# A graph-network kernel on one core: layer 0's mask bytes written to DRAM by casting transfers instead of GpSimd casts

## The chip, the core and the metric

The kernel runs on one core of one Trainium2 chip, as one launch. The metric is the device time of that launch in microseconds, the median of several runs. A profile of one execution, taken by the hardware profiler, goes with it.

The engines are named as the profile names them: PE is TensorE (matmuls; PEld is its weight loads), DVE is VectorE, ACT is ScalarE, POOL is GpSimd, SP is SyncE, which here only issues DMAs. "q" after an engine's name is its instruction queue. The DMA queue of GpSimd is q0 (software_dynamic), that of SyncE is q1 (hardware_dynamic); both are served by the same 16 DMA engines.

## The reference

`x` is 2708 x 512 float32, `adj` is a symmetric 2708 x 2708 matrix of zeros and ones with about 16 ones in a row. Four layers follow one another, each of the form `x = layernorm(x + layer(x, adj))`:

```python
deg = max((adj != 0).sum(-1), 1)
# layer 0
pooled = (dinv * (adj + I) * dinv) @ x + x        # dinv = rsqrt(deg)
relu(pooled @ W + b)
# layer 1
dis = (adj.sum(1) + 1e-8) ** -0.5
(dis * adj * dis) @ x @ W.T + b
# layer 2: twice
Wh, Ws = split(x @ W)
a = softmax(Wh @ Ws.T) * adj
leaky_relu(a @ Wh + x)
# layer 3
adj @ (H @ W) + b
```

## The kernel before

The 2708 nodes are cut into 22 blocks of 128 rows (the last has 20), and the columns of the transposed adjacency matrix into six chunks `CH` of 512, 512, 512, 512, 384 and 276 columns. The 22 blocks of a chunk go in six groups `GROUPS` of 4, 4, 4, 4, 3 and 3 blocks. Layers 0, 1 and 3 multiply by the adjacency matrix in steps (layer, chunk, group): for each block j of the group, a 128-row piece of `x`, split into a high part `xh` and a rest `xl`, is the stationary operand, and the piece `m` of `adj.T` (128 rows, one chunk of columns) is the moving one. The products of a chunk gather in four PSUM banks `acc`. Layer 2 is the attention. It has its own loops and uses the stored masks too.

The order of instructions on each engine is the order in which the program issues them; it is written out by hand, by `Run.seq` and `step`. `step` of a group first calls `before_products`, which issues the loads of the group two steps ahead (`load`), the preparation of the next group (`prepare`), and at two places the column sums (`degrees`). Then it issues the matmuls of the group (`multiply`). After the last group of a chunk come `degrees` and `evict`. The chunk's second product (`project`, matmuls into `mm`), its end and its layernorm (`ends`) are spread over the steps of the next chunk.

What layer 0 does with a block of `adj.T`:

- `load`: SyncE loads it as float32 into a tile `at`, one of eleven wide buffers. In chunk 0 GpSimd also loads the block of `x`; in the third group of each chunk it loads four tiles `xt` of the transposed input.
- `prepare`: ScalarE splits `x` into `xh` (`halve`, chunk 0 only; VectorE makes `xl`), and casts `at` to the moving operand `m`.
- `examine`: ScalarE casts two blocks `at` into one bfloat16 tile `some`; VectorE compares every block with itself (`odd`, with a count of the entries that are not zero or one) and adds the pair to a running sum `part`. The bytes of the group are stored in DRAM, in `masks[k]`, laid out as 128 partitions x 22 blocks x chunk width. Layers 1 to 3 load their adjacency from there, at a quarter of the bytes.
- `degrees`: after the last block VectorE adds the halves of `part` (`both`), TensorE sums them over the partitions (`deg`, `cnt`), VectorE makes `dg` and from `cnt` in a string of small instructions (`rs_v`, `rs_y`, `rs_t`) `dis` and `rdeg`; GpSimd multiplies the four tiles `xt` by `dg`.
- `evict`: VectorE adds `acc` and `xt` into `ht`, the stationary operand of `mm`.

The storing of the bytes, before: for each pair of blocks GpSimd casts `some` to a `uint8` tile `bytes`; after the group's pairs, one DMA issued by GpSimd stores the tile. GpSimd's queue at the start therefore holds, in order: loads of `x` for the first groups, constants, and then for each group its two casts, the store, the loads of `x` of a later group, and between them the loads of `xt`, of the weights `w` and of the bias.

Nearly all SBUF tiles come from one pool of 82 pages, each as large as 128 x 512 float32; a tile takes a free page when it is made, and waits for that page's last user. `bytes`, `some`, `odd` and `part` are pages, the `at` tiles are not.

All instructions are recorded through one wrapper, so that most of the profile's rows show its line, L70, and have to be told apart by the tiles' names.

Of the kernel before, what the change touches and what calls it, by code (L numbers as in the profile page):

```python
# [12 lines left out]
U8 = mybir.dt.uint8  # L13
# [6 lines left out]
P = 128  # L20
# [4 lines left out]
DC = D // P  # L25
BANK = 512
# [487 lines left out]
class Fast:  # L514
# [299 lines left out]
    def examine(self, ly, k, g, ats):  # L814
        nc, cw = self.nc, CH[k][1]
        b0 = GROUPS[g][0]
        if g == 0:
            ly.part[k] = self.page(f"part{k}", BF, (P, 2, BANK))
        odd = self.page(f"odd{k}_{g}", BF)
        at_b = self.page(f"bytes{k}_{g}", U8, (P, DC, BANK))  # L820
        for q in range(0, len(ats), 2):
            some = self.page(f"some{k}_{g}_{q}", BF, (P, 2, BANK))
            m = min(2, len(ats) - q)
            for h in range(m):
                at = ats[q + h][:, :cw]
                n = k * NB + b0 + q + h
                nc.scalar.copy(some[:, h, :cw], at)
                nc.vector.scalar_tensor_tensor(
                    odd[:, :cw],
                    at,  # L830
                    1.0,
                    at,
                    ALU.is_equal,
                    ALU.not_equal,
                    accum_out=self.k.bad[:, n : n + 1],
                )
            nc.gpsimd.tensor_copy(at_b[:, q : q + m, :cw], some[:, :m, :cw])

            n = QW if b0 + q == NB - 1 else P
            p, t = ly.part[k][:n, :m, :cw], some[:n, :m, :cw]  # L840
            if b0 + q == 0:
                nc.vector.tensor_copy(p, t)
            else:
                nc.vector.tensor_add(p, p, t)
        nc.gpsimd.dma_start(
            self.k.masks[k][:, b0 : b0 + len(ats), :], at_b[:, : len(ats), :cw]
        )

    def multiply(self, ly, k, g, only=None, ds=range(DC)):
        nc, cw = self.nc, CH[k][1]  # L850
# [993 lines left out]
```

## Time and profile before

| what | value |
|---|---|
| median of 3 runs | 2369.26 us (2368.26 to 2371.22) |
| the profiled execution: time / span | 2338.2 us / 2336.5 us |
| mean granted TensorE clock in it | 0.993 |
| layer 0, from the first instruction to its last mask store | about 0 to 316 us |
| GpSimd casts `bytes<-some` | 72, 75.4 us |
| GpSimd DMA issues `mask<-bytes` | 36, 22.3 us |
| time from issue to landing of these | 2.3 to 5.7 us, median 3.6 |
| DMA of the whole kernel | 463.5 MB, mean 198 GB/s |

The profile's times come from its one execution; its own time stands beside its span. A row of a group names the engine, the operation, the tiles (out<-in) with their shapes and count, then the busy time in microseconds and the mean of one in nanoseconds, and after the bar the idle time ahead of the group and what ended it. A row of the waits reads: engine, tile and line, then what it waited for, the total in microseconds, the number of times and the longest. A row of stages gives for each engine the busy microseconds and the number of instructions.

### The profile page before, as it was taken

The numbers are of one execution on the slowest core, as the hardware profiler recorded it, in microseconds if no ns is written. First come the engines' busy times: TensorE is split into PE (matmuls) and PEld (weight loads), VectorE is DVE, ScalarE is ACT, GpSimd is POOL, SyncE is SP. The second block draws the span as 40 slices with busy tenths as digits, with TensorE's granted clock in tenths as the row PEclk, the third lists the DMA queues.
The fourth block names the chain that finished last, engine by engine and source line by source line (L and its number), as shares of the span: only waits on it lengthen the run. The fifth ranks groups of instructions, "written<-read, shape, count | busy, mean of one in ns | idle before, by whom it ended". The sixth has DMA issues, their size and how long they took to land.

```text
span 2336.5 us, 26171 instructions
## 1 busy us (share of the span) xinstructions
PE 2274.8 (97%) x8518; PEld 1292.5 (55%) x8518; DVE 1474.8 (63%) x2831; ACT 662.2 (28%) x1334; POOL 762.3 (33%) x879
## 2 busy tenths in 40 slices
PE   8999999999999999999999999999999999999997
PEld 6677677778644444443456444444443456566585
DVE  6999986786655529657677511228677788724523
ACT  6544353223100113222223200113232334432211
POOL 6645641111000000636375550000636466551000
PEclk9999999999999999999999999999999999999998
DMA  9765652222434404869699996405869799983311
GB/s 343 258 199 169 182 172 86 74 86 70 171 146 167 154 0 143 278 229 311 204 324 350 302 388 232 152 0 163 279 217 314 233 316 329 305 279 96 123 48 43
DMA packets 312440, 463.50 MB, mean 198 GB/s; under 512 B 60162, under 2 KB 189706, under 8 KB 312292
## 3 DMA queue, kind: packets, MB, share of 16 engines
q1 hardware_dynamic: 252276, 240.81, 31.5%
q0 software_dynamic: 60016, 220.92, 27.1%
q8 instruction: 69, 1.13, 0.2%
q14 instruction: 79, 0.65, 0.1%
HBM read 307.75 MB, written 153.85 MB: 198 GB/s over the span
## 4 chain that ended last, share of the span: by engine, by line
PE 84%; DVE 7%; DMA 4%; issue 2%; ACT 1%; POOL 1%; SPq 0%; DVEq 0%; ACTq 0%; POOLq 0%
PE sp L70 32%; PE acc L70 29%; PE mm L70 9%; PE z L70 6%; PE wst L70 6%; DMA pairs<-s 1%; DMA at<-in_adj_t 1%; DVE st L70 1%; DMA at<-mask 1%; ACT m L70 1%; DVE s L70 1%; PE list L70 1%; PE mix L70 0%; POOL bytes L70 0%; PE tr_x2t L70 0%
## 5 line engine op out<-in xcount | busy, mean ns | idle before, releaser
L70 POOL DMA_INDIRECT g<-pairs,givers x510 | 516.2, 1012 | 897.0 <-DMA pairs<-s 537.4
L70 PE MATMUL sp<-xs,wst_sb 128*128 128x512 f32 (+3 forms) x2112 | 797.7, 544 | 0.0
L70 PEld LDWEIGHTS sp<-xs,wst_sb 128*128 128x128 f32 (+1 forms) x2112 | 380.0, 186 | 406.8 <-issue 321.9
L70 PE MATMUL acc<-m,xh 128*128 128x512 f32 (+4 forms) x1584 | 571.4, 382 | 13.6 <-ACT m L70 7.0
L70 PE MATMUL acc<-m,xl 128*128 128x512 f32 (+4 forms) x1584 | 553.2, 367 | 1.5 <-DVE xl L70 1.5
L70 PEld LDWEIGHTS acc<-m,xh 128*128 128x128 f32 (+1 forms) x1584 | 290.3, 189 | 81.4 <-issue 22.3
L70 PEld LDWEIGHTS acc<-m,xl 128*128 128x128 f32 (+1 forms) x1584 | 290.3, 189 | 48.1 <-issue 5.7
L70 ACT COPY s<-sp 128x512 f32<-128x512 f32 (+2 forms) x252 | 133.6, 531 | 482.1 <-PE sp L70 469.5
L70 PE MATMUL acc<-g 128*32 128x512 f32 (+1 forms) x1020 | 260.8, 605 | 0.9 <-DMA g<-pairs,givers 0.5
L70 DVE TENSOR_TENSOR top<-top,s 128x512 f32<-128x512 f32 (+5 forms) x240 | 149.6, 623 | 170.6 <-ACT s L70 169.1
L70 PE MATMUL mm<-w,ht 128*128 128x512 f32 (+1 forms) x528 | 222.6, 593 | 8.1 <-DVE ht L70 8.1
L70 ACT CAST m<-at 128x512 fp32r<-128x512 uint8 (+5 forms) x396 | 199.2, 567 | 80.0 <-DMA at<-mask 63.7
L70 ACT ACTIVATE s<-s 128x512 f32<-128x512 f32 (+3 forms) x264 | 150.7, 580 | 236.6 <-DVE s L70 236.3
L70 DVE TENSOR_TENSOR sum<-sum,s 128x512 f32<-128x512 f32 (+4 forms) x252 | 157.4, 625 | 23.9 <-ACT s L70 23.9
L70 DVE TENSOR_TENSOR s<-s,a 128x512 f32<-128x512 f32 (+3 forms) x264 | 165.9, 628 | 10.2 <-DMA a<-mask 1.2
L70 DVE TENSOR_TENSOR s<-s,shift 128x512 f32<-128x512 f32 (+3 forms) x264 | 162.8, 620 | 6.7 <-ACT shift L70 6.7
L70 PEld LDWEIGHTS mm<-w,ht 128*128 128x128 f32 (+1 forms) x528 | 95.5, 186 | 124.4 <-issue 110.9
L70 PE MATMUL wst<-xt,mixed 128*128 128x512 f32 (+2 forms) x384 | 152.5, 550 | 1.7 <-ACT mixed L70 1.7
L70 PEld LDWEIGHTS acc<-g 128*32 128x32 f32 (+1 forms) x1020 | 75.4, 134 | 136.9 <-issue 115.8
L70 PE MATMUL z<-w,xt 128*128 128x512 f32 (+1 forms) x352 | 151.0, 596 | 0.0
L70 DVE COPY z_sb<-z 128x512 f32<-128x512 f32 (+1 forms) x44 | 30.3, 690 | 179.5 <-PE z L70 176.3
L70 POOL DMA_DIRECT2D x<-o x44 | 26.0, 596 | 358.0 <-DVE o L70 354.2
(167 smaller groups left out, 1657.4 us busy)
## 6 DMA issues: line engine op xcount, KB each, us to landing
pairs<-s SPq DMA_DIRECT2D x378, 128.0 KB
pairs<-z_sb SPq DMA_DIRECT2D x84, 512.0 KB
at<-in_adj_t SPq DMA_DIRECT2D x84, 256.0 KB
xres<-x POOLq DMA_DIRECT2D x44, 256.0 KB, 4.3
x<-o POOLq DMA_DIRECT2D x43, 256.0 KB, 3.1
x<-x SPq DMA_DIRECT2D x37, 256.0 KB
at<-mask SPq DMA_DIRECT2D x32, 256.0 KB
xt<-t SPq DMA_DIRECT2D x32, 256.0 KB
```

The source lines that it names most:

```text
L70: ins = call(*args, **kw)
```

## The change

In `examine` the tile of bytes is no longer made, and GpSimd's cast is gone. In its place GpSimd issues a DMA for each pair of blocks straight from the bfloat16 tile `some` to the `uint8` tensor in DRAM; the transfer converts each element. The store of the whole group behind the loop is gone. So a group has two transfers where it had one, each of two blocks (or one, where a group has three).

```diff
@@ examine
         odd = self.page(f"odd{k}_{g}", BF)
-        at_b = self.page(f"bytes{k}_{g}", U8, (P, DC, BANK))
         for q in range(0, len(ats), 2):
             some = self.page(f"some{k}_{g}_{q}", BF, (P, 2, BANK))
...
-            nc.gpsimd.tensor_copy(at_b[:, q : q + m, :cw], some[:, :m, :cw])
+
+            nc.gpsimd.dma_start(
+                self.k.masks[k][:, b0 + q : b0 + q + m, :], some[:, :m, :cw]
+            )
...
                 nc.vector.tensor_add(p, p, t)
-        nc.gpsimd.dma_start(
-            self.k.masks[k][:, b0 : b0 + len(ats), :], at_b[:, : len(ats), :cw]
-        )
```

## The prediction, made before the change was run

> **What bounds the kernel now.** I read the page's engine shares first, then the waits of TensorE, then the stage in which the edited function runs (layer 0, up to about 320 us), and there the wait that ends last.
>
> ```profile
> PE 2274.8 (97%) x8518; PEld 1292.5 (55%) x8518; DVE 1474.8 (63%) x2831; ACT 662.2 (28%) x1334; POOL 762.3 (33%) x879
> PE 84%; DVE 7%; DMA 4%; issue 2%; ACT 1%; POOL 1%; SPq 0%; DVEq 0%; ACTq 0%; POOLq 0%
> ```
>
> TensorE (PE) fills 97% of the span and 84% of the chain; GpSimd (POOL), from which the change takes work, carries 1% of the chain. So the change is worth what it does to TensorE's few gaps. The waits of TensorE from 0 to 60 us, and then from 60 to 360 us:
>
> ```profile
> PE mix L70 <- DMA wt<-in_w_t: 4.3, 1, 4.3
> PE acc L70 <- ACT m L70: 3.5, 2, 2.9
> ```
>
> ```profile
> PE mm L70 <- DVE ht L70: 5.5, 3, 2.3
> PE acc L70 <- DVE dg L70: 3.6, 1, 3.6
> PE acc L70 <- DVE xl L70: 1.2, 1, 1.2
> ```
>
> That is all that can come back: 2.95 us at 59.2 (m late), then 2.26, 1.25 and 1.95 us at 75.8, 235.1 and 279.8 (ht late), and 3.57 us at 312.95 (dg late). The table of stages says what stands behind them (TensorE, weight loads, VectorE (DVE), ScalarE (ACT), POOL, granted clock, DMA share, GB/s):
>
> ```profile
> 21.00:24.00 3.00, 3.00 (x14) 2.44 (x14) 2.96 (x6) 3.00 (x7) 2.70 (x4) 1.00 0.30 100
> 24.00:39.00 15.00, 15.00 (x68) 12.40 (x67) 14.86 (x29) 12.05 (x25) 11.79 (x20) 1.00 0.99 346
> 39.00:50.00 11.00, 11.00 (x49) 8.81 (x47) 10.15 (x15) 6.74 (x14) 8.88 (x11) 1.00 1.04 398
> 61.00:64.20 3.20, 3.20 (x9) 2.52 (x8) 3.10 (x6) 3.20 (x7) 2.69 (x4) 0.50 1.01 362
> 116.00:172.00 56.00, 56.00 (x231) 39.82 (x230) 53.52 (x105) 23.55 (x46) 28.26 (x35) 1.00 0.62 196
> 313.40:317.00 3.60, 3.60 (x11) 2.77 (x10) 2.19 (x7) 3.60 (x7) 2.84 (x6) 0.53 0.96 356
> ```
>
> Three things are to be seen. From 24 to 60 us the DMA engines are full; that is what the first gap waits for. Later the DMA is at 0.62 and VectorE is the runner-up, busy 53.5 of 56 us. And after the two longest gaps (2.95 and 3.57 us) the granted clock is halved for some 3.5 us, so each costs about 1.8 us more than itself; the shorter ones cost nothing further.
>
> VectorE's groups up to 345 us, and the tile odd alone:
>
> ```profile
> L70 DVE SCALAR_TENSOR_TENSOR odd<-at 128x512 bf16<-128x512 f32 x88 | 88.1, 1001 | 1.4
> L70 DVE TENSOR_TENSOR part<-part,some 128x1024 bf16<-128x1024 bf16 x36 | 34.6, 961 | 0.2 <-ACT some L70 0.2
> ```
>
> ```profile
> L70 DVE SCALAR_TENSOR_TENSOR odd<-at x132: 431/688/3196, 19.1 to 305.6; 128x512 bf16<-128x512 f32 x88, 128x384 bf16<-128x384 f32 x22, 128x276 bf16<-128x276 f32 x22
> ```
>
> The first gives a mean of 1001 ns, the second the spread over all widths; at 512 columns the undisturbed ones take 0.69 us. In the timeline the long ones (1.52 us at 21.63, 1.53 at 26.83, 1.40 at 28.40) each lie beside a GpSimd cast; one at 23.20, beside GpSimd's DMA issues, takes 0.69.
>
> **What the Trainium skill says.** "SBUF — State Buffer", Who interferes with whom: a VectorE instruction with two SBUF inputs contends with a GpSimd instruction that reads SBUF, and one holds the shared ports for the whole instruction. odd reads at twice and part reads part and some, so the trace agrees (0.69 against 1.40 to 1.53). "DMA: Bandwidth & Descriptors", SWDGE vs HWDGE vs iDMA: a casting transfer must be issued from GpSimd; that is where the diff has it. It states no rate for a cast, and this trace holds no casting transfer. "TensorE: Matmul & The Clock Gate", Part 1: about 3.4 us of idleness halves the clock. The trace agrees roughly (2.95 us did, 2.26 did not).
>
> **The change part by part.**
>
> *GpSimd.* Gone: 72 casts (48.3 + 8.7 + 8.4 + 7.4 + 1.7 + 0.9 = 75.4 us), 36 issues (22.3 us) and 33 waits of 0.3 us for the last cast (9.8 us). New: 72 issues, one for each some tile (six groups of two in six chunks), at the 619 ns that a mask issue takes now: 45 us. Together 53 us less work and 10 us less waiting. Each waits for ScalarE's some, as the cast did. What stands behind it on GpSimd (loads of x, xt and w, the xt*dg products, stores of o) moves forward. GpSimd is 33% busy: nothing on the path by itself.
>
> *VectorE.* Relief: odd 88 x (1001-685) = 27.8, 22 x (811-555) = 5.6, 22 x (555-440) = 2.5; part 36 x (961-685) = 9.9, then 1.5 and 0.9; the first copies and one both about 3. Together some 51 us of 300. It lies beside TensorE everywhere but at the gaps:
> - 75.8 us: dg starts at 68.86 though its sum deg was there at 65.9, since two odd and a copy (1.53, 1.40, 1.25 against 0.69, 0.69, 0.42) run long beside casts, 2.4 us in all. ht comes that much sooner: **-2.0** (0 to -2.3).
> - 235.1 and 279.8 us: dg follows its sum within 0.6 us, so VectorE is not behind; what holds ht is the chain of small instructions beside the xt*dg products on GpSimd, which stay. **0**.
> - 312.95 us: VectorE runs without a break from 298.7; beside the last casts two odd (0.89, 1.00 against 0.45), two part (0.87, 0.73 against 0.44, 0.29) and both (0.58 against about 0.3) lose 2.2 us. What is late next is ScalarE's xh (last at 307.1), then xl, feeds and dg by order: dg at about 310.3. The gap falls to 1.3 us and the clock stays up: -2.2 - 1.8 = **-4.0** (0 to -4.2).
>
> *DMA.* The same bytes are written, but read at two bytes each. Before 60 us there are 4.75 transfers of 256 KB; read as 512 KB they add 1.25 MB, at 390 KB/us **+3.2 us** of a full resource, if a cast runs at the rate of its read side. If it counts by what it writes, 0; if a cast is slower, more: unknown, taken from 0 to four times the time per byte read. Against it: the hole at 21 to 24 us (DMA at 0.30) is there because the x loads stand behind two casts and one issue until 23.47; then they leave at about 21.65 (the second some ends at 21.06, and one issue follows), **-1.8 us**. The next ones leave earlier too (at 27.9 for 31.5, as some ends at 27.3, and at some 37 for 42.7), and ScalarE's waits for x of 2.95 and 2.58 us, which feed the gap at 59.2, shrink: I take **-1.4**, since other loads then come later. Start-up: **0** (-4.7 if the gap at 59.2 closes and the clock holds).
> After 60 us each group has 9.2 us and the DMA 40% to spare: a doubled mask transfer (+0.65 us) hides there.
>
> *Pages.* bytes goes, which frees a page a group; some is now held until its transfer lands (bytes took 2.3 to 5.7 us) instead of to the sum. Whoever takes the page next waits: before, four w loads did so once, 2.4 us on GpSimd. 82 pages go round; I take 0, with 2 us either way.
>
> **Sum:** -2.0 - 4.0 + 0 = -6.0 us on the profiled execution (2338.2 us, span 2336.5): 2332. The median of the runs shown, 2369.26, is 31 us above it; the gaps should be alike, so 2369.3 - 6 = **2363**.
>
> **The rivals.** *A slow cast* (slower). If the inline cast runs at a quarter of the rate, a mask group takes 5.2 us instead of 0.65 on engines that are full: 4.75 x 4.5 = 21 us more before 60 us, less 1.8, 1.4 and the 6.0 after: +12, 2381; more if at loads fall behind later too, where 4.5 us in 9.2 fills the spare 40%. The x loads stand behind it in GpSimd's own queue, which makes it worse. For it: DMA at 0.99 to 1.04 there. Against: nothing shows such a rate. The sign turns at (6.0 + 1.8 + 1.4) / 4.75 = 1.94 us more a group, 2.6 us in all, which is half the rate per byte read; 3.6 us in all make it slower than a measurement can miss.
> *The relief doesn't reach TensorE* (no change). Another VectorE delay (feeds, 2.28 us, stands ahead of dg by order) holds the 312.95 gap near 3 us, the clock is halved anyway, and the start pays 1.5 us: -2.0 - 0.6 + 1.5 = -1, 2368. For it: the chain around 235 and 280 is just of this kind.
> *The start is GpSimd's order* (faster still). If the x loads were what starved ScalarE, the gap at 59.2 closes with its slow clock: -6 - 4.7 = -11, 2358.
> That the casts stay somewhere else is excluded by the diff.
>
> **How the numbers follow.** My forecast 0.32, faster still 0.12, no change 0.25, slow cast 0.31. A change of 0.2%, 4.7 us, is about what a measurement of this kernel can tell from none; my forecast is just beyond it. So faster has 0.42, the first two less what falls into the middle, same 0.26, slower 0.32. The range goes from the faster still, 2357, to beyond the slow cast, 2388, and leaves out the worst casts. The forecast's own range is 2359 to 2366.
>
> **What would show it.** In the profile after: odd 128x512 at a mean near 700 ns and part near 690; POOL busy lower by some 53 us up to 345; mask<-some with landing times near the 3.6 us of now (slow cast: 8 or more); no TensorE wait for dg over 1.5 us, and clock 1.00 behind it; the wait of acc for m near 59 us not above 3 us. I am wrong if the DMA share stays at 1 past 65 us, if new waits of ScalarE for mask transfers appear, or if the dg gap stays.

## The result and the profile after

The change makes the kernel slower: 2378.96 us (median of 11 runs, 2365.62 to 2384.49) against 2368.26 us for the kernel before beside it. The ratio is 1.0036 with an interval of 1.0018 to 1.0054; three more measurements gave 1.0037, 1.0036 and 1.0036. The prediction was 2363 us, so it had the sign wrong (6 us less foretold, some 10 us more measured), although the time lies in its range. The profiled execution took 2371.86 us (span 2370.1). The one profiled before, 2338.2 us, was 30 us quicker than its kernel's median; profiled again beside the first experiments, the kernel before took 2371.43 us, and in one set of runs its median was 2340.41 us. The same chip number stands beside that quicker set and two of the slower ones, so what makes this difference is not known. Whole spans of different profiles therefore say little here. Stages can be compared.

The engines and the chain of the profile after:

```profile
PE 2286.4 (96%) x8518; PEld 1295.2 (55%) x8518; DVE 1419.8 (60%) x2831; ACT 660.3 (28%) x1334; POOL 710.0 (30%) x843
PE 82%; DVE 7%; DMA 4%; issue 3%; ACT 1%; another core or an unknown queue 1%; POOL 1%; SPq 0%; DVEq 0%; ACTq 0%; POOLq 0%
```

VectorE lost 55.0 us of work (1474.8 to 1419.8) and GpSimd 52.3 us (762.3 to 710.0), as foreseen. VectorE's groups up to 345 us and the tile odd alone (the last row gives the shortest, median and longest in ns) say that the relief is complete:

```profile
L70 DVE SCALAR_TENSOR_TENSOR odd<-at 128x512 bf16<-128x512 f32 x88 | 60.5, 687 | 1.4
L70 DVE TENSOR_TENSOR part<-part,some 128x1024 bf16<-128x1024 bf16 x36 | 24.7, 685 | 0.0
L70 DVE SCALAR_TENSOR_TENSOR odd<-at x132: 433/683/695, 19.8 to 302.2; 128x512 bf16<-128x512 f32 x88, 128x384 bf16<-128x384 f32 x22, 128x276 bf16<-128x276 f32 x22
```

No odd is long any more: the longest takes 695 ns where one took 3196. The waits of TensorE, from 0 to 60 us and from 60 to 360 us:

```profile
PE mix L70 <- DMA wt<-in_w_t: 4.2, 1, 4.2
PE acc L70 <- DVE xl L70: 0.8, 1, 0.8
PE acc L70 <- ACT m L70: 0.6, 2, 0.4
```

```profile
PE acc L70 <- DVE dg L70: 4.3, 1, 4.3
PE acc L70 <- ACT m L70: 3.6, 1, 3.6
PE mm L70 <- DVE ht L70: 2.7, 2, 1.5
PE acc L70 <- DVE xl L70: 1.2, 1, 1.2
```

The wait of acc for m of 3.6 us in the second list is the first gap, 2.95 us before: it ends at 61.1 us now, so it has changed lists but has not closed, and the clock is halved with it, from 59.5 to 66.3 us. mm waits for ht twice instead of three times: in this profile the gap at 75.8 us is gone. But the wait for dg, which was to fall to 1.3 us, has grown from 3.57 to 4.3 us. The table of stages (PE, weight loads, DVE, ACT, POOL, granted clock, DMA share, GB/s):

```profile
21.00:24.00 3.00, 3.00 (x15) 2.46 (x14) 2.97 (x9) 3.00 (x7) 2.63 (x5) 1.00 0.90 206
24.00:39.00 15.00, 15.00 (x68) 12.43 (x67) 13.03 (x29) 12.72 (x25) 10.25 (x20) 1.00 1.02 350
116.00:172.00 56.00, 56.00 (x231) 39.80 (x230) 40.98 (x97) 23.31 (x46) 18.12 (x28) 1.00 0.73 210
313.40:317.00 3.60, 3.60 (x9) 2.83 (x10) 1.51 (x9) 3.51 (x8) 3.59 (x7) 0.50 0.92 332
```

The hole in the DMA at 21 to 24 us has closed (0.30 to 0.90), VectorE has 15 us to spare in 56 where it had 2.5, and the clock behind the dg gap is still halved, here from 312.1 for 6.8 us.

**Why dg is still late** stands in the timelines (start, duration, instruction; in brackets the idle time before it and what ended it). First VectorE in the kernel before, then VectorE and ScalarE in the changed one:

```profile
306.96 0.58 DVE L70 TENSOR_TENSOR both<-part 128x276 bf16<-128x276 bf16 x1
307.46 2.88 DVE L70 SCALAR_TENSOR_TENSOR xl<-x,dis,xh 128x512 fp32r<-128x512 f32 x4
310.27 2.28 DVE L70 TENSOR_REDUCE feeds<-at 128x64 bf16<-128x2048 uint8 x1
312.46 0.43 DVE L70 TENSOR_SCALAR dg<-deg 128x276 f32<-128x276 f32 x1
```

```profile
303.12 0.30 DVE L70 TENSOR_TENSOR both<-part 128x276 bf16<-128x276 bf16 x1
303.33 1.41 DVE L70 SCALAR_TENSOR_TENSOR xl<-x,dis,xh 128x512 fp32r<-128x512 f32 x2
308.43 0.75 DVE L70 SCALAR_TENSOR_TENSOR xl<-x,dis,xh 128x512 fp32r<-128x512 f32 x1 [3.69 <-DMA mask<-some]
309.84 0.75 DVE L70 SCALAR_TENSOR_TENSOR xl<-x,dis,xh 128x512 fp32r<-128x512 f32 x1 [0.66 <-ACT xh L70]
310.51 2.29 DVE L70 TENSOR_REDUCE feeds<-at 128x64 bf16<-128x2048 uint8 x1
312.70 0.44 DVE L70 TENSOR_SCALAR dg<-deg 128x276 f32<-128x276 f32 x1
```

```profile
308.56 0.62 ACT L70 CAST m<-at 128x512 fp32r<-128x512 uint8 x1 [4.12 <-DMA mask<-some]
```

VectorE comes to the last of its share in this chunk (both) at 303.12, before at 306.96. Then it must write xl of layer 1 into a page that a mask transfer still reads, and stands until 308.43; ScalarE's m waits for another such page. feeds and dg follow by order. What VectorE was ahead by, 3.8 us, the two pages took back. The three other profiles of the changed kernel show the same two waits (2.6 to 4.1 us for xl, 4.0 to 4.6 us for m). GpSimd's timeline says why the transfers land so late:

```profile
298.01 2.13 POOL L70 DMA_DIRECT2D x<-x  x4
300.13 1.45 POOL L70 DMA_DIRECT2D mask<-some  x2
302.25 0.56 POOL L70 DMA_DIRECT2D x<-x  x1 [0.67 <-PE acc L70]
```

Both are issued by 301.58, behind four x loads; the 276-byte packets that they write run from 304.6 to 308.1 us. From 298 to 308 us the DMA share is 1.04 (before: 0.89). Before, such a page was free as soon as GpSimd's cast and VectorE's sum had read it; what waited for the landing was the page of bytes.

### The profile page after: what moved, and what is told of

Its sections match the earlier page's. It is cut to its first block, busy times and chain, and to the rows that moved or that the text cites. A ratio compares the mean times of both kernels' runs of the same rounds, so it can differ in the third digit from the quotient of the medians.

```text
span 2370.1 us, 26150 instructions
## 1 busy us (share of the span) xinstructions
PE 2286.4 (96%) x8518; PEld 1295.2 (55%) x8518; DVE 1419.8 (60%) x2831; ACT 660.3 (28%) x1334; POOL 710.0 (30%) x843
## 3 DMA queue, kind: packets, MB, share of 16 engines
q1 hardware_dynamic: 252276, 240.81, 30.9%
## 4 chain that ended last, share of the span: by engine, by line
PE 82%; DVE 7%; DMA 4%; issue 3%; ACT 1%; another core or an unknown queue 1%; POOL 1%; SPq 0%; DVEq 0%; ACTq 0%; POOLq 0%
PE sp L70 30%; PE acc L70 29%; PE mm L70 9%; PE z L70 6%; PE wst L70 6%; DMA at<-in_adj_t 2%; DMA pairs<-s 1%; DVE s L70 1%; DMA mask<-some 1%; DVE r L70 1%; DVE st L70 1%; DMA g<-pairs,givers 1%; DVE at_row L70 1%; PE list L70 1%
## 5 line engine op out<-in xcount | busy, mean ns | idle before, releaser
L70 POOL DMA_DIRECT2D x<-o x44 | 25.9, 596 | 356.6 <-DVE o L70 356.6
```

The costliest lines, as they stand in the source:

```text
L70: ins = call(*args, **kw)
```

## The experiments

Each kernel was timed together with the kernel before. That one has a median of 2368 to 2370 us beside all of them but four; beside those four, called the quicker set below, it has 2340.41. Because the order of TensorE's matmuls is the same in all kernels, the time between two given matmuls can be compared; this table shows it as a difference from the first profile of before, in us, for single profiled executions. The bounds are the times of those matmuls in that first profile.

| kernel | 4 to 78 | 78 to 306 | 306 to 321 | 321 to 421 | sum to 421 | after 421 |
|---|---|---|---|---|---|---|
| before, again | 3.0 | 0.2 | -0.3 | -0.8 | 2.0 | 31.3 |
| before, 40 transfers later | 1.2 | -0.4 | 0.8 | 0.0 | 1.6 | 30.8 |
| before, 36 transfers later | 0.9 | -0.4 | 0.0 | 0.0 | 0.5 | 30.5 |
| after, mean of 4 profiles | -1.4 | -0.2 | 1.5 | -0.6 | -0.7 | 36.8 |
| before with a transfer a pair | 2.0 | 8.5 | 1.0 | -0.8 | 10.7 | 46.7 |
| after with the casts kept | 4.3 | 0.5 | 2.8 | -0.8 | 6.6 | 42.1 |
| after, last chunk without casting | -0.8 | -0.4 | -3.2 | -0.8 | -5.3 | 35.3 |
| bytes written by ScalarE | 2.0 | -0.5 | -3.1 | -0.8 | -2.4 | 28.1 |
| the same, a transfer a pair | 3.3 | -0.4 | -0.3 | -0.8 | 1.7 | 25.9 |
| before, 36 small transfers in layer 0 | 1.8 | 0.9 | -0.4 | 0.0 | 2.3 | 34.7 |
| after, 4 small transfers more | 1.3 | -0.5 | 3.9 | -0.8 | 3.7 | 37.1 |

The last column's 30 us is mostly the difference between that first execution and the slower sets; only differences between its rows count. Single profiles scatter: the four of the changed kernel lie between 0.3 and 2.4 in the third column and between 32.7 and 42.5 in the last.

**The kernels themselves.** Two controls, the kernel before and the kernel after, each once more:

> The kernel before, unchanged, against itself, with a new profile. Theory A (layer 0's gain and its new costs cancel, and what differs between the two profiles at 1195 to 1330 and 1890 to 2130 us is the scatter of stretches in which the DMA engines are full): the ratio is 1.000 within 0.003, the matmuls up to 660 us lie within 1 us of the first profile of before, and the later stretches scatter by 10 us or more, so that the span comes nearer to 2360 than to 2336. Theory B (the change itself lengthens the attention by some 15 us or more): the span is again near 2337 and the two stretches are as in the first profile.

> The changed kernel again. Both theories: the ratio to before is between 1.002 and 1.006. Theory A: layer 0 and 1 end within 1 us of the first profile of after (PE at 660 us some 0.5 us later than before), the attention scatters. Theory B: the attention is again 15 us longer than in the first profile of before.

Measured: 2367.28 us, ratio 0.9994 (0.9977 to 1.0011), and 2378.74 us, 1.0037 (1.0022 to 1.0053). The kernel before repeats itself in time (by 421 us its profile is 2.0 us from the first one, not within the 1 us expected), and so does the loss.

**One transfer a pair, casts kept.** The kernel before; the group's store is cut into the pairs' stores:

```diff
             nc.gpsimd.tensor_copy(at_b[:, q : q + m, :cw], some[:, :m, :cw])
+            nc.gpsimd.dma_start(
+                self.k.masks[k][:, b0 + q : b0 + q + m, :], at_b[:, q : q + m, :cw]
+            )
...
-        nc.gpsimd.dma_start(
-            self.k.masks[k][:, b0 : b0 + len(ats), :], at_b[:, : len(ats), :cw]
-        )
```

> Before with the casts and the byte tile kept, but the store of a group cut into one plain transfer for each pair of blocks: 72 transfers, as after, none of them casting. If the number of transfers in GpSimd's queue is what costs (each transfer waits for an earlier one of its queue to land), the ratio is about 1.002 to 1.005 and x<-x and x<-in_x show such waits; if it is the casting transfer's time on the engines or the pages of some held until it lands, the ratio is 1.000 to 1.001.

Measured: 2390.67 us, 1.0080 (1.0055 to 1.0105). No byte is cast by a transfer here, and it is slower than the change and than either forecast; nor do loads of x show the waits that the forecast named. 8.5 of the 22 us lie between 78 and 306 us. VectorE's sums there, in the kernel before and in this one (up to 345 us):

```profile
L70 DVE TENSOR_TENSOR part<-part,some 128x1024 bf16<-128x1024 bf16 x36 | 36.8, 1022 | 0.1
```

```profile
L70 DVE TENSOR_TENSOR part<-part,some 128x1024 bf16<-128x1024 bf16 x36 | 41.2, 1144 | 0.0
```

Beside the extra stores VectorE's sums take longer; with odd (1001 to 1047 ns) that is 8.4 us more work on an engine that was busy 53.5 of 56 us, and mm then waits 8.0 us for ht between 78 and 306 us instead of 2.8. That the stores push the casts to where VectorE sums is the likely reason, not a tested one. This part needs the casts, which the changed kernel doesn't have. A larger part, some 16 us (46.7 against the controls' 30.9), lies after 421 us, and its cause is open. So the loss can't be read as the price of the transfers in the changed kernel.

**The casts kept beside the casting transfers.** The kernel after, with GpSimd's casts into a tile that nobody reads:

```diff
+        at_b = self.page(f"bytes{k}_{g}", U8, (P, DC, BANK))
...
+            nc.gpsimd.tensor_copy(at_b[:, q : q + m, :cw], some[:, :m, :cw])
```

> After with GpSimd's casts kept too (into the tile of bytes, which nothing reads): the casting transfers without the relief for VectorE. If the relief is worth the 2.4 us at 75 us and little else, the time is 2 to 4 us above after (ratio to before 1.005 to 1.007), odd 128x512 has its mean of about 1000 ns again. If the relief brings nothing to the end, the ratio is that of after.

Measured: 2386.85 us, 1.0066 (1.0040 to 1.0091): the casts cost some 8 us when they stand beside the new transfers, where 2 to 4 were expected. The relief is worth something; the change pays more than that for it.

**The bytes written by ScalarE.** No bfloat16 tile, no cast on GpSimd, one plain transfer a group:

```diff
+        at_b = self.page(f"bytes{k}_{g}", U8, (P, DC, BANK))
...
-                nc.scalar.copy(some[:, h, :cw], at)
+                nc.scalar.copy(at_b[:, q + h, :cw], at)
...
-            p, t = ly.part[k][:n, :m, :cw], some[:n, :m, :cw]
+            p, t = ly.part[k][:n, :m, :cw], at_b[:n, q : q + m, :cw]
...
+        nc.gpsimd.dma_start(
+            self.k.masks[k][:, b0 : b0 + len(ats), :], at_b[:, : len(ats), :cw]
+        )
```

> ScalarE casts each block straight to a uint8 tile of the whole group (no bfloat16 tile some), VectorE's sums read that tile, and one plain transfer a group stores it, as in the kernel before. GpSimd's casts are gone, the number of transfers is that of before, none casts. Theory A and B alike: the relief without the doubled transfers, -6 to -8 us, 2360 to 2363. Theory C, the loss of the changed kernel comes from GpSimd running ahead once its casts are gone (its loads and stores collide with others): 2375 to 2380 here too. Against all of them: if VectorE's sums of uint8 take longer than those of bfloat16 (690 ns for 128x1024), or a ScalarE write of uint8 is slower than one of bfloat16, the time rises with that.

> ScalarE writes the uint8 tile itself, one plain transfer a group, no cast on GpSimd (as before). Its median was 2.6 us below the kernel before. Theory A (the doubled number of transfers is what the changed kernel pays for): again 0 to 6 us below the kernel before, and 8 to 14 us below the changed kernel. Theory C (the loss comes with GpSimd running ahead): near the changed kernel on a chip where that one loses 10.

Measured: 2337.81 us in the quicker set, 0.9985 (0.9976 to 0.9995), then 2365.13 us, 0.9986 (0.9974 to 0.9998), 13 us below the changed kernel beside it. It is the quickest kernel of the study, though by less than hoped. TensorE's waits from 60 to 360 us in the second of them:

```profile
PE mm L70 <- DVE ht L70: 5.0, 3, 2.3
PE acc L70 <- DVE dg L70: 2.5, 2, 2.2
PE acc L70 <- DVE xl L70: 1.2, 1, 1.2
```

The wait for dg falls to 2.2 us and the clock stays at 1.00 behind it. ht still waits at 75.8 us, because this kernel's sums read uint8: part takes 1220 ns here against 685 in the changed kernel. VectorE is relieved of 26.8 us (1474.8 to 1448.0) instead of 55.0, and dg at this place starts at 69.52, no sooner than before (68.86).

**The last chunk without casting.** The changed kernel; only in the last chunk ScalarE writes the bytes and one plain transfer a group stores them, with the lines of the experiment above:

```diff
+        if k == 5:
+            at_b = self.page(f"bytes{k}_{g}", U8, (P, DC, BANK))
...
+        else:
             for q in range(0, len(ats), 2):
                 some = self.page(f"some{k}_{g}_{q}", BF, (P, 2, BANK))
```

> The changed kernel, but in the last chunk (276 columns) ScalarE writes the uint8 tile itself and one plain transfer a group stores it: the 60 other transfers still cast. In the changed kernel VectorE's xl and ScalarE's m wait at 308 us for pages that casting transfers still hold, and TensorE waits 4.3 to 5 us for dg at 313. Theory P (the held page is what keeps that gap): the wait for dg falls to about 1.3 us and the time by 3 to 5 us against the changed kernel. Theory D (another wait takes its place, or the gap is VectorE's own): gap 3 us or more, time as the changed kernel's.

> The changed kernel again, beside the three others on the same chip. All theories: above the kernel before by 5 to 10 us if this chip is like the one of its first two measurements (+10), by about 4 us if it is like the one on which it ran with four tiny DMAs (+4).

Measured: 2369.85 us, 1.0005 (0.9988 to 1.0022), beside 2378.20 us, 1.0036 (1.0018 to 1.0054), for the changed kernel: 8.4 us back from one chunk in six. The two intervals against the kernel before still touch; set against each other, the 14 runs of each kernel have means 7.4 us apart, give or take 4.4, so the gain is clear and its size is not. TensorE's wait for dg, then VectorE's timeline, in the first of the two:

```profile
PE acc L70 <- DVE dg L70: 2.0, 1, 2.0
```

```profile
304.84 0.30 DVE L70 TENSOR_TENSOR both<-part 128x276 bf16<-128x276 bf16 x1
305.06 2.73 DVE L70 SCALAR_TENSOR_TENSOR xl<-x,dis,xh 128x512 fp32r<-128x512 f32 x4
307.71 2.28 DVE L70 TENSOR_REDUCE feeds<-at 128x64 bf16<-128x2048 uint8 x1
309.91 0.43 DVE L70 TENSOR_SCALAR dg<-deg 128x276 f32<-128x276 f32 x1
```

The four xl follow each other without a wait. both comes later than in the changed kernel (304.84 for 303.12), and dg all the same earlier (309.91 for 312.70). The stage from 306 to 321 us is 4.7 us shorter than in the changed kernel's four profiles, and the clock there is not halved. The rest of the 8.4 us lies elsewhere and is not explained. Theory P stands for the wait; for the time it promised 3 to 5 us. The edit also halves the transfers of that chunk and the pages that they hold (one a group, where two `some` were held), so it shows the price of all this at this place, not of the cast alone.

**Two plain transfers a group without any cast.** As the kernel with ScalarE's bytes, but a store for each pair:

```diff
+            nc.gpsimd.dma_start(
+                self.k.masks[k][:, b0 + q : b0 + q + m, :], at_b[:, q : q + m, :cw]
+            )
```

> ScalarE writes the uint8 tile itself as in r3_bytes_direct, but with a plain transfer for each pair of blocks: 72 transfers, no cast anywhere, and no bfloat16 page. With 36 transfers it stood 0.14% (3.3 us) below the kernel before. Theory Q (the doubled number costs through GpSimd's queue in layer 0, and the casts' absence makes room for it): 0 to 3 us above r3_bytes_direct, so -3 to 0 against the kernel before. Theory T (72 transfers cost by themselves, wherever GpSimd stands): +8 to +15 against r3_bytes_direct, so +5 to +12.

Measured: 2372.19 us, 1.0008 (0.9990 to 1.0027): 0.22% or some 5 us more than with one transfer a group, between theory Q (0 to 3) and theory T (8 to 15). The two ratios come from different sets and their intervals just touch. In its profile 2.8 us of that lie at 306 to 321 us, where VectorE again waits for a mask transfer (1.1 us). So at this place a second plain transfer costs 2.8 us and casting 1.8 more (-3.1, -0.3 and 1.5 in the table), in single profiles.

**More transfers elsewhere.** The kernel before with 40, then 36 transfers of 64 KB near the end of layer 1, and with 36 of 512 bytes in layer 0, one behind the first cast of a group:

```diff
                 self.ends(run, g)
+                if g == 0:
+                    for n in range(40):
+                        nc.gpsimd.dma_start(kernel.dump[n], kernel.ones)
```

```diff
             nc.gpsimd.tensor_copy(at_b[:, q : q + m, :cw], some[:, :m, :cw])
+            if q == 0:
+                i = 6 * k + g
+                nc.gpsimd.dma_start(self.k.dump[i : i + 1, :], self.k.ones[:1, :])
```

> The kernel before, with 40 extra GpSimd DMAs of 64 KB (ones to an unread DRAM tensor) not in layer 0 but near the end of layer 1, where GpSimd is idle for 30 to 45 us between stores; 40 is a multiple of 8. Theory A1 (the extra transfers cost only where layer 0 needs GpSimd's next instruction): as the kernel before, within 2 us. Theory A2 (more transfers in GpSimd's queue disturb the later stages, whatever the place): +3 to +8 us, lost after 1250 us.

> The kernel before with 36 GpSimd DMAs of 64 KB near the end of layer 1, where GpSimd is idle; with 40 at this place it took 2 us more than the kernel before. Theory B: +8 to +12 us. Theory N: +1 to +3 us as with 40.

> The kernel before with its casts and its 36 stores, and a 512-byte GpSimd DMA behind the first cast of each group: as many more instructions in GpSimd's queue in layer 0 as in r1_split, but almost no bytes, and the stores stay whole. Theory Q: layer 0 loses 8 to 12 us as in r1_split, at the waits of mm for ht, and the time rises by 10 to 20. Theory T: 0 to +4, as with 36 or 40 transfers at the end of layer 1.

Measured: 2370.54 us, 1.0013 (1.0000 to 1.0027); 2372.03 us, 1.0020 (1.0008 to 1.0033); 2375.14 us, 1.0020 (1.0001 to 1.0039). Thirty-six to forty more GpSimd transfers cost 2 to 5 us at both places, and neither theory of the last two had that. A shift by four places adds nothing that can be told from none.

**The shift by four places.** Four transfers of 512 bytes make the extra ones a multiple of 8, or shift the kernel before alone:

```diff
+        if 1 <= k <= 4 and g == 0:
+            nc.gpsimd.dma_start(self.k.dump[k - 1 : k, :], self.k.ones[:1, :])
```

> The kernel before with four extra GpSimd DMAs of 512 bytes (a row of ones to an unread DRAM tensor), one at the first group of each of the chunks 1 to 4; nothing else. It moves every later GpSimd DMA by four places, as the 36 extra transfers of the changed kernel do (36 is 4 more than a multiple of 8, and each GpSimd DMA waits for the one eight before it). Theory A, the number of transfers in layer 0 costs: 4/36 of 16 to 19 us, so +2 us, about 2370. Theory B, the later stages lose because other transfers now stand eight places apart: +8 to +16 us, 2377 to 2385, with the loss after 450 us.

> The kernel before with its casts kept and a plain transfer for each pair (72 transfers), and the four tiny DMAs as well: 40 extra, a multiple of 8, so that the later GpSimd DMAs stand as in the kernel before. Theory A: as without the tiny ones, 2390 to 2393. Theory B: only what layer 0 and 1 lose stays, some 5 to 9 us, 2374 to 2378.

> The changed kernel with the four tiny DMAs, 40 extra in all. Theory A: no better than the changed kernel, 2379 to 2381. Theory B: it loses the later stalls and keeps the relief of VectorE, 2360 to 2370.

> The changed kernel with four 512-byte GpSimd DMAs more in layer 0: 40 extra, a multiple of 8. Theory B (the shift by four places costs some 10 us in the later stages): 2366 to 2370 where the kernel before has 2368, that is 8 to 12 us below the changed kernel. Theory N (not the shift): within 3 us of the changed kernel, +7 to +12 against the kernel before.

> The kernel before with its casts and a plain transfer for each pair, and the four tiny DMAs. Theory B: only the 9 to 12 us that layer 0 loses remain of the 22, 2377 to 2381 where the kernel before has 2368. Theory N: 2388 to 2393.

> The changed kernel again on this chip, for the comparison with the four tiny DMAs: +10 us against the kernel before where that has 2368 us; where it has 2340 us, theory B expects about 10 us, and a theory in which the chip decides about 4 us.

Measured: in the quicker set before with them 2340.88 us, 1.0001 (0.9990 to 1.0011), the pairs' kernel with casts 2355.30 us, 1.0059 (1.0044 to 1.0074), the changed one 2344.67 us, 1.0015 (1.0005 to 1.0024). In a slower set the changed one 2375.05 us, 1.0027 (1.0012 to 1.0042), beside 2376.52 us, 1.0036 (1.0022 to 1.0050), without them, the pairs' kernel 2388.16 us, 1.0074 (1.0047 to 1.0100). Theory B promised 8 to 16 us for the shift; the shift alone cost nothing, and taking it away gave about 2, within the noise: it falls. In the quicker set every kernel's loss came out smaller; why is not known.

## Why the prediction was wrong

**VectorE's relief: right.** 51 us were foreseen and 55 came; odd and part stand at 687 and 685 ns, as the nearest undisturbed instructions had said. That also agrees with what the prediction took from the Trainium skill, "SBUF — State Buffer", Who interferes with whom: with GpSimd's casts gone, no odd is held any longer. **GpSimd:** 53 us less work foreseen, 52.3 measured.

**The gap at 75.8 us: about right.** -2.0 us (0 to -2.3) was said; by 78 us, at the matmul behind the gap, the four profiles of the changed kernel are 0.1, 1.5, 1.9 and 2.2 us ahead of the first profile of before. In the first of them the gap is gone partly because TensorE came 2.4 us later, out of the longer first gap and its slow clock; in another a gap of 1.74 us stayed. The gap was also worth more than the prediction thought. It read from its one trace that a gap of 2.26 us leaves the clock up, but of the eleven profiles, of all kernels, with a gap of 2.24 to 2.29 us at this place, nine show the clock halved for 3.4 us behind it. Such a gap is shorter than the 3.4 us of idleness that the prediction quotes; here the measurement decides. The gaps at 235 and 280 us stayed, as said.

**The rate of the cast: the right end, too low.** A written packet of 1024 bytes took 98 ns in the mean (96 in the median), where plain packets of 4096 bytes in GpSimd's queue took 159 in the median. A group of four blocks has 256 of the first, 256 x 98 / 16 = 1.57 us of the 16 engines, instead of 64 x 159 / 16 = 0.64: +0.93 us, where +0.65 was assumed and the slow-cast rival needed +4.5. That rival is dead. At the start the sum of nothing held: ahead of the gap at 75.8 us, at 73 us, TensorE was 0.5 us behind the first profile in the mean of four, and the controls 0.9 to 1.8. But the first gap did not shrink; it is 2.8 to 3.6 us long.

**The gap at 312.95 us: the step that failed.** The prediction took -4.0 us from it (-2.2 and the slow clock's -1.8). The stage from 306 to 321 us became 1.4 us longer than in the controls (1.5 against their mean of 0.1). Its first half was right: VectorE did finish 3.8 us earlier. So was its price of the slow clock: in the two kernels that bring the gap to 2.0 and 2.2 us, the clock stays up and the matmuls behind the gap take 1.6 us less. The fault is in the paragraph on pages, which wrote down that some is held until its transfer lands, and that whoever takes the page next waits, and then took 0, with 2 us either way. The waits that followed are of 3.69 us (VectorE) and 4.12 us (ScalarE), and two of the signs that it had named for being wrong came: new waits of ScalarE for mask transfers, and a dg gap that stays. Three things, as far as the traces show, made it more than 2 us at this place. The transfers stand behind the x loads in GpSimd's queue, which runs earlier now. The last chunk's casts are the dearest for their bytes: 512 packets of 276 bytes at 43 ns are 1.38 us a group, where the plain transfer's 32 of 4140 bytes (about 167 ns) and 16 of 552 (37 ns) are 0.37. And the two pages are taken next by xl and m of layer 1, which stand ahead of dg. Without casts in that chunk the stage is 3.2 us shorter than in the first profile: close to the -4.0 that the relief was to bring.

Elsewhere too the mask transfers land later. The rows of the DMA issues (count, size, and last the median us from issue to landing) are from the kernel before and then the changed one, each with four small transfers more, in the quicker set; the chunks of 512 columns come first, then 384, and in the second 276:

```profile
mask<-bytes POOLq DMA_DIRECT2D x16, 256.0 KB, 3.4
mask<-bytes POOLq DMA_DIRECT2D x12, 192.0 KB, 2.8
```

```profile
mask<-some POOLq DMA_DIRECT2D x40, 128.0 KB, 5.6
mask<-some POOLq DMA_DIRECT2D x10, 96.0 KB, 4.8
mask<-some POOLq DMA_DIRECT2D x10, 69.0 KB, 6.0
```

Half the bytes take 5.6 us instead of 3.4: the prediction's test of "near 3.6 us" failed here.

**"72 issues: nothing on the path": wrong by 2 to 5 us.** The number of transfers was costed at nothing. With no cast anywhere, one transfer a pair costs 0.22% (5 us) more than one a group, and 36 to 40 more in the kernel before cost 2 to 5 us. How they cost it is shown only in part: the 2.8 us at 306 to 321 us.

**The sum** then reads, from the ratios: relief with one plain transfer -3.3 us (0.9986, with half of VectorE's relief), doubled transfers +5 (to 1.0008), casting from held pages +7 (to 1.0036), together +8.5. The last term is what is left, so the sum comes out by itself. The kernel that casts in five chunks of six stands at 1.0005, which points to the last chunk for most of that term. Each term is sure to some 3 or 4 us. The rival "the relief doesn't reach TensorE" had the right place, the dg gap and its halved clock, but feeds as its reason and no price for the page.

**What stays open.** By 421 us TensorE in the changed kernel is about 2 us ahead of the controls (-0.7 against their mean of 1.4), yet its median is some 10 us behind. So the step that failed, 5.5 us of the forecast at 312.95 us, tells why little was won by then; that the sign turned is not explained by it alone. In the profiles some 6 us are lost after 421 us (36.8 against 30.9), and 5 in the quicker set with four small transfers in both kernels (4.7 against -0.7), most of it around the end of the attention, which runs with nearly full DMA engines and scatters by several us in every kernel. The program there is the same. The shift by four doesn't explain it. The number of transfers may in part: 36 small ones in layer 0 give 34.7 there, but 36 or 40 later ones 30.5 and 30.8. Single profiles are too coarse to say more. The prediction's sum has no term for it.

## What to carry over

When a store is made to read the working tile itself, the tile is held until the transfer lands: list who takes its buffer next, and price that wait at the place where the DMA engines are fullest, not at the mean landing time. In this kernel the place to look was the last stage before a hand-over between layers, since there the next layer's first tiles stand ahead of the instruction that TensorE waits for. Doubling the number of transfers had a price, here 2 to 5 us, even where the issuing engine is idle 70% of the time, and taking work from the runner-up engine pays only where the next wait in line is shorter.

## What the runs showed of the hardware

- A casting transfer from bfloat16 to bytes took 98 ns in the mean for a written packet of 1024 bytes, 50 for 384 and 43 for 276; plain packets of 4096 bytes in the same queue took 159 in the median.
- A VectorE sum of 128x1024 took 685 ns with both inputs bfloat16 and 1220 ns with one of them uint8; a ScalarE cast of 128x512 to uint8 took 616 ns, as to bfloat16 (615).
- The same kernel had medians of 2340.41 and 2368.39 us in two sets of runs with the same chip number, 1.2% apart; in the profiles nearly all of the difference lies after 421 us.
- In the first 420 us of these traces the granted clock is halved for 3.4 or 6.8 us at a time: after the 3.57 us gap of the kernel before for 3.4 us, after the 4.3 us gap of the changed one for 6.8 us, and not at all after those of 2.0 and 2.2 us at the same place. After a gap of 2.24 to 2.29 us at 75 us it was halved in nine profiles of eleven.
